# Centring a weight ahead of block sums, later bias loads, and a plan chosen from twelve

## The chip, the cores and the metric

The kernel runs on one core of a Trainium2 chip. The metric is the device time of one execution in microseconds (us). A profile of one execution says what each engine did and when. The engines are TensorE (PE, with its weight loads as PEld), VectorE (DVE), ScalarE (ACT), GpSimd (POOL) and SyncE (SP, which only issues transfers here).

## The reference

Four layers work on x of shape (64, 256, 128) with one adjacency matrix of 256 x 256. Each adds its result to its input and takes a layer norm over the last axis of 128.

```python
# layer 0: sum over powers of adj, seven weights
x = _layernorm(x + _L0(x, adj, adj, weight_1))     # x_all = [x, A x, A^2 x, A^3 x, A x, A^2 x, A^3 x]; einsum('bnik,iok->bno')
# layer 1: adj @ (x @ weight) + bias
x = _layernorm(x + _L1(x, adj, weight, bias))
# layer 2: (D^-1/2 (adj + I) D^-1/2) @ x @ W.T + b
x = _layernorm(x + _L2(x, adj, W, b))
# layer 3: five steps of a gated recurrent cell, two messages through adj
for _ in range(5):
    av = concat(adj @ h, adj @ h); u3 = h @ u3_w.T + u3_b
    z = sigmoid(av @ w3_w.T + w3_b + u3); r = sigmoid(av @ w4_w.T + w4_b + u3)
    hv = tanh(av @ w5_w.T + w5_b + (r * h) @ u5_w.T + u5_b)
    h = (1 - z) * h + z * hv
x = _layernorm(x + h)
```

All values are float32.

## The kernel before

The batch of 64 is cut into 32 groups of two (`NB`). A group's values carry the number of its first batch element: x_4 is the input of the third group. Within a group every layer follows the other; across groups twelve may be in work at once (`ACTIVE`). A value of a group is a tile of 128 x 512.

Nothing is written in a fixed order. Each piece of work is recorded as an `Op` with an engine, an assumed cost, an assumed lag until its result can be used, a rank, and a function that emits its instructions. `Plan.order` (L84) is a list scheduler: among the pieces whose inputs are assumed to be there, it takes the one that can start first and, among equals, the one of lower rank. A group's rank is its number (L468), for the last seven groups (`LEVEL`) a closer spaced one that grows with each piece; the weights' preparation has ranks of its own, from -9 to 2.1, the first argument of `pre` (L217), `fetch` (L224) and `load` (L228). The resulting list is the instruction order of each engine. Each engine takes its instructions strictly in that order and waits at the first whose inputs are missing. SP is such a queue as well: a transfer behind one that still waits is not issued. A transfer from SP uses one of eight semaphores in turn, so the ninth waits until the first has landed.

The head of the program, which the change touches, holds these pieces:

- PE warms up on transposes (L254), turns the adjacency matrix to `aT` (L270) and squares it (L277, `p_a`, copied by ACT to `a2T`, L284). The first two groups (x_0, x_2) take plain products with `a2T` and turn x on PE; the later ones use seven block products in place of eight (`seven`, L704), for which POOL forms differences (L724 to L732: `tsq`, `tqq`) and DVE adds up the parts (L751 to L761, with `mq` as the result).
- `w0s` (L291 to L296) are the sums of the seven slices of W_0 that belong to equal powers. `centre` (L300) takes the mean over the output channels off a weight, so that a later layer norm needs no mean. The centred `w0s` is what the first weight products (`py`, L565 to L597) read. `w0_blocks` (L311) forms differences of it.
- `aTp` is a copy of `aT` with its rows in another order, made by four transfers on SP (L324). `block_sums` (L359) forms five sums of a matrix's four blocks on DVE, for `aT`, `a2T`, the normalised `anT`, and `aTp`.
- `wb` (L380 to L386) holds the weight of layer 1 and the two biases, all centred by one call of `centre`. Both biases are loaded from POOL's queue (L385), behind a small DVE copy `made` that gives `wb` its first writer; six further bias columns `braw` follow on the same queue (L421).
- For group 2 on, x is turned by DVE (`tx`, L852), stored (`dx`, L855) and read back (`xT`, L860). The load of a group's x (L843) may be issued only after the first piece of the group two before it.

Of the kernel before, what the change touches and what calls it, by code (L numbers as in the profile page):

```python
# [1 line left out]

# [8 lines left out]
OP = mybir.AluOpType  # L11
AX = mybir.AxisListType

P = 128
# [3 lines left out]
LEVEL = 7  # L18
# [9 lines left out]
class Val:  # L28
# [3 lines left out]
    def __init__(self, kind, shape, name, nb=NB):  # L32
        self.kind, self.shape, self.name, self.nb = kind, shape, name, nb
        self.writers, self.readers, self.users = [], [], []
        self.slot = self.tile = None
# [15 lines left out]
class Plan:  # L51
# [3 lines left out]

    def __init__(self, slots):
        self.ops, self.slots = [], slots

    def add(self, engine, cost, lag, rank, run, reads=(), writes=(), after=(), joint=False):

# [18 lines left out]
        self.ops.append(op)  # L81
        return op

    def order(self):  # L84
        free = {}
        pool = {k: [(0.0, i) for i in range(n)] for k, n in self.slots.items()}
        left = {op: len(op.deps) for op in self.ops}
        placed = {op: [v for v in op.vals if v.kind != "const"] for op in self.ops}
        after = {op: [] for op in self.ops}
        for op in self.ops:  # L90
            for d in op.deps:
                after[d].append(op)
        open_ = {}
        ready = {}
        for op in self.ops:
            if not left[op]:
                ready.setdefault(op.engine, []).append((0.0, op))
        done = []
        while any(ready.values()):
            best = None  # L100
            for e, waiting in ready.items():
                t0 = free.get(e, 0.0)
                pick = None
                for at, op in waiting:
                    need, opens = {}, 1
                    for v in placed[op]:
                        if v.slot is None:
                            need[v.kind] = need.get(v.kind, 0) + 1
                        elif v.kind == "bank":
                            opens = 0  # L110
                    short = False
                    for k, n in need.items():
                        if len(pool[k]) < n:
                            short = True
                            break
                        at = max(at, sorted(pool[k])[n - 1][0])
                    if short:
                        continue
                    key = (max(at, t0), opens, op.rank, op.seq)
                    if pick is None or key < pick[0]:  # L120
                        pick = (key, op)
                if pick and (best is None or pick[0] < best[0]):
                    best = pick
            assert best, "the plan is stuck"
            (start, *_), op = best
            ready[op.engine] = [w for w in ready[op.engine] if w[1] is not op]
            op.start, op.end = start, start + op.cost + op.lag
            free[op.engine] = start + op.cost
            for v in placed[op]:
                if v.slot is None:  # L130
                    pool[v.kind].sort()
                    v.slot = pool[v.kind].pop(0)[1]
                    open_[v] = len(v.users)
                open_[v] -= 1
                if not open_[v]:
                    pool[v.kind].append((max(u.end for u in v.users), v.slot))
            for n in after[op]:
                left[n] -= 1
                if not left[n]:
                    at = max(d.end for d in n.deps)  # L140
                    ready.setdefault(n.engine, []).append((at, n))
            done.append(op)
        assert len(done) == len(self.ops)
        return sorted(done, key=lambda op: (op.start, op.seq))


def pe_cost(columns, n=1):
    return n * 2 * (max(columns, P) / 1.2 + 2)
# [11 lines left out]
def kernel(  # L160
# [30 lines left out]
    nc = tc.nc  # L191
    B, N, C = x.shape
    T = N // P
    G = B // NB
# [8 lines left out]
    SHAPES = {"bank": [P, 512], "x": [P, 512], "w": [P, 512], "th": [P, 384], "q": [P, P], "h": [P, 256], "st": [P, Q * 6], "mv": [P, Q * 2],  # L203
              "ve": [P, Q], "rs": [P, Q]}
    slots = {"bank": BANKS, "x": ACTIVE + 3, "w": 38, "th": 12, "q": 12, "h": 21, "dram1": 8, "dram2": 16, "st": 12, "mv": 12, "ve": 24, "rs": 12}
    plan = Plan(slots)


    def constant(name, shape):
# [7 lines left out]
    def pre(rank, engine, cost, run, reads=(), writes=(), lag=None, joint=False, after=()):  # L217
        lag = lag or {"SP": 2300, "PE": 260, "DVE": 260, "ACT": 130, "POOL": 100}[engine]
        return plan.add(engine, cost, lag, rank, run, reads, writes, after, joint)
# [3 lines left out]

    def fetch(rank, o, src, v, queue, after=()):  # L224
        e, cost = QUEUES[queue]
        return pre(rank, queue, cost, lambda: e.dma_start(o, src), [], [v], lag=8000, joint=True, after=after)

    def load(rank, name, shape, src, keep=True, queue="SP", lag=2300):  # L228
        v = constant(name, shape) if keep else Val("w", shape, name)
# [4 lines left out]
    ident = const.tile([P, P], F32, name="ident")  # L234
# [10 lines left out]
    warm = temp("warm")  # L245
# [4 lines left out]
    def warming(n):  # L250
        for i in range(n):
            nc.tensor.transpose(warm.ap[:, (i % 4) * P:(i % 4 + 1) * P], ident, ident)
# [4 lines left out]
    a_nat = load(-9, "a_nat", [P, T, N], adj.rearrange("(t p) m -> p t m", p=P), False)  # L257
    aT, a2T = constant("aT", [P, T, N]), constant("a2T", [P, T, N])
    p_at, p_a2, p_an = temp("p_at"), temp("p_a2"), temp("p_an")
# [17 lines left out]
    def square():  # L277
        for mt in range(T):
            for kt in range(T):
                mm(p_a2.ap[:, mt * N:(mt + 1) * N], a_nat.ap[:, kt, mt * P:(mt + 1) * P], aT.ap[:, kt, :],  # L280
                   kt == 0, kt == T - 1)

    pre(-8, "PE", pe_cost(N, 4), square, [a_nat, aT], [p_a2])
    pre(-8, "ACT", act_cost(512), lambda: nc.scalar.copy(flat(a2T), p_a2.ap), [p_a2], [a2T])  # L284


# [2 lines left out]
    w0s = constant("w0s", [P, 4, C])  # L289
# [9 lines left out]

    def centre(v, means):  # L300
        nc.vector.reduce_sum(means.ap, v.ap, axis=AX.X)
        nc.vector.tensor_scalar(means.ap, means.ap, -1.0 / C, None, op0=OP.mult)
        nc.vector.tensor_tensor(v.ap, v.ap, means.ap[:, :, None].to_broadcast(v.ap.shape), op=OP.add)

    w0m = constant("w0m", [P, 4])
    pre(-7, "DVE", 1500, lambda: centre(w0s, w0m), [w0s], [w0s, w0m])


    w0t = constant("w0t", [P, 4, C])
# [6 lines left out]
        nc.vector.tensor_sub(t3, w_3, w_1)  # L316
        nc.vector.tensor_sub(t4, w_2, t2)

    pre(1.2, "DVE", 1000, w0_blocks, [w0s], [w0t])


    aTp = constant("aTp", [P, T, N])
# [8 lines left out]
    ahat, anT = Val("w", [P, T, N], "ahat"), constant("anT", [P, T, N])  # L331
# [24 lines left out]

    sums_of = {}

    def block_sums(rank, name, aTs):  # L359
        v = constant(f"s_{name}", [P, 5, P])  # L360
        a11, a12, a21, a22 = (aTs.ap[:, kt, t * P:(t + 1) * P] for t in range(T) for kt in range(T))

        def run():
            nc.vector.tensor_add(v.ap[:, 0, :], a21, a22)
            nc.vector.tensor_sub(v.ap[:, 1, :], v.ap[:, 0, :], a11)
            nc.vector.tensor_sub(v.ap[:, 2, :], a11, a21)
            nc.vector.tensor_sub(v.ap[:, 3, :], a12, v.ap[:, 1, :])
            nc.vector.tensor_scalar(v.ap[:, 4, :], a22, -1.0, None, op0=OP.mult)

        pre(rank, "DVE", 1200, run, [aTs], [v])  # L370
        sums_of[aTs] = v

    block_sums(0.6, "aT", aT)
    block_sums(0.6, "a2T", a2T)
    block_sums(0.6, "anT", anT)
    block_sums(0.7, "aTp", aTp)

    wb, wbm = constant("wb", [P, 3, C]), constant("wbm", [P, 3])  # L380

    made = pre(-9, "DVE", 100, lambda: nc.vector.tensor_copy(wb.ap[:, 1:3, 0], ident[:, :2]), [], [wb])
    fetch(0.6, wb.ap[:, 0, :], w1, wb, "SP")
    for i, b in ((1, b1), (2, b2)):
        last = fetch(0.1, wb.ap[:, i, :], bass.AP(tensor=b.tensor, offset=b.offset, ap=[[0, P], [1, C]]), wb, "POOL", (made,))  # L385
    pre(0.9, "DVE", 1100, lambda: centre(wb, wbm), [wb, w0s], [wb, wbm])  # L386
    w1c, b1c, b2c = ((wb, wb.ap[:, i, :]) for i in range(3))
    raw = {name: load(0.6, f"raw_{name}", [P, src.shape[1]], src, False, lag=9000)
# [29 lines left out]
    braw, bsum = constant("braw", [P, 6]), constant("bsum", [P, 3])  # L418

    for i, src in enumerate((w3_b, w4_b, w5_b, u3_b, u3_b, u5_b)):  # L420
        fetch(0.2, braw.ap[:, i:i + 1], src.rearrange("(p o) -> p o", o=1), braw, "POOL", (last,))  # L421
    pre(0.4, "DVE", 150, lambda: nc.vector.tensor_add(bsum.ap, braw.ap[:, :3], braw.ap[:, 3:]), [braw], [bsum])
    zb, rb, hb = ((bsum, bsum.ap[:, i:i + 1]) for i in range(3))

# [24 lines left out]
    class Group:  # L449
        def __init__(self, start, nb):  # L450
            self.start, self.nb, self.first, self.last = start, nb, None, None
            self.gate = self.load_gate = ()
            self.count = 0
            self.q, self.width = nb * T, nb * N

            self.by_tile = (lambda v: v.ap.rearrange("p (k q i) -> p q k i", k=4, q=self.q),
                            lambda v: v.ap.rearrange("p (q k i) -> p q k i", k=4, q=self.q))
# [532 lines left out]
```

## Time and profile before

| what | us |
|---|---|
| three timed runs | 1344.65, 1346.7, 1347.05 (median 1346.7) |
| the profiled execution | 1345.33 |
| its span, first to last instruction | 1343.5 |
| mean granted TensorE clock | 0.996 |

The span is a little shorter than the execution's own time, since what lies around the first and last instruction is not in it. Below, every point in time is counted from the span's start. A row of instructions in order of time gives its start, its length, engine, line and operation, the tile written and the tiles read; in brackets stands how long the engine was idle before it and what ended that. The length of a DVE or ACT row holds some overlap with the next one, so the distance of two starts is the better price of an instruction in a row. A float32 matmul stands as two records, a transpose as one.

### The profile page before, as it was taken

The numbers are of one execution on the slowest core, as the hardware profiler recorded it, in microseconds if no ns is written. First come the engines' busy times: TensorE is split into PE (matmuls) and PEld (weight loads), VectorE is DVE, ScalarE is ACT, GpSimd is POOL, SyncE is SP. The second block draws the span as 40 slices with busy tenths as digits, with TensorE's granted clock in tenths as the row PEclk, the third lists the DMA queues.
The fourth block names the chain that finished last, engine by engine and source line by source line (L and its number), as shares of the span: only waits on it lengthen the run. The fifth ranks groups of instructions, "written<-read, shape, count | busy, mean of one in ns | idle before, by whom it ended". The sixth has DMA issues, their size and how long they took to land.

```text
span 1343.5 us, 22696 instructions
## 1 busy us (share of the span) xinstructions
PE 1326.7 (99%) x6913; PEld 931.0 (69%) x6913; DVE 1046.2 (78%) x2579; ACT 773.2 (58%) x2361; POOL 638.2 (48%) x998
## 2 busy tenths in 40 slices
PE   8999999999999999999999999999999999999997
PEld 6987756667677877766666767766666787666554
DVE  6976767879886978777779796986886778777776
ACT  3677645544556666554655656565555588544445
POOL 4887633434355746352535465353343476322212
PEclk8999999999999999999999999999999999999999
DMA  5521323534242333343524332333332213433323
GB/s 154 147 67 57 86 85 90 156 89 133 81 130 75 102 88 110 95 118 87 157 74 131 100 107 70 105 116 99 106 95 80 70 57 118 122 90 94 89 85 102
DMA packets 269305, 134.87 MB, mean 100 GB/s; under 512 B 175712, under 2 KB 240864, under 8 KB 269184
## 3 DMA queue, kind: packets, MB, share of 16 engines
q1 hardware_dynamic: 268928, 133.29, 34.4%
q8 instruction: 55, 0.90, 0.3%
q14 instruction: 66, 0.54, 0.1%
q0 software_dynamic: 256, 0.13, 0.1%
HBM read 67.31 MB, written 65.80 MB: 99 GB/s over the span
## 4 chain that ended last, share of the span: by engine, by line
PE 95%; DVE 2%; ACT 1%; DMA 1%; issue 0%; SPq 0%; POOLq 0%; POOL 0%; DVEq 0%; ACTq 0%
PE pr L201 30%; PE ph L201 20%; PE pmg L201 19%; PE py L201 11%; PE pm L201 7%; PE pz L201 4%; PE pmq L201 3%; DMA x<-in_x_dram 1%; PE s L201 1%; ACT y L524 0%; DVE s L546 0%; DVE tx L852 0%; DVE ss L619 0%; ACT y L539 0%; DMA aTp<-aT 0%
## 5 line engine op out<-in xcount | busy, mean ns | idle before, releaser
L201 PE MATMUL pr<-mg,w435u5T 128*128 128x512 f32 x640 | 322.3, 593 | 0.0
L725 POOL TENSOR_TENSOR tsg<-h 128x256 f32<-128x256 f32 x128 | 95.2, 743 | 285.5 <-DMA h<-dh 202.1
L528 POOL TENSOR_TENSOR rs<-ve,half 128x4 f32<-128x4 f32 x99 | 101.3, 1023 | 205.4 <-ACT y L524 169.0
L831 ACT ACTIVATE pr<-pr,bsum 128x512 f32<-128x512 f32 x160 | 105.6, 660 | 137.7 <-PE pr L201 137.2
L831 ACT ACTIVATE r<-pr,bsum 128x512 f32<-128x512 f32 x160 | 105.4, 659 | 127.2 <-PE pr L201 124.9
L524 ACT ACTIVATE y<-s,root 128x128 f32<-128x128 f32 x396 | 153.7, 393 | 17.3 <-DVE s L546 15.7
L201 PE MATMUL pr<-hT,w2u3T 128*128 128x512 f32 x320 | 163.0, 593 | 0.0
L201 PE MATMUL ph<-mg,w435u5T 128*128 128x512 f32 x320 | 162.9, 593 | 0.0
L201 PE MATMUL ph<-rh,w435u5T 128*128 128x512 f32 x320 | 162.8, 593 | 0.0
L838 DVE TENSOR_TENSOR d<-ph,hT 128x512 f32<-128x512 f32 x160 | 109.5, 685 | 67.4 <-ACT ph L831 66.8
L201 PEld LDWEIGHTS pmg<-aTp,h 128*128 128x128 f32 x512 | 91.9, 196 | 74.4 <-issue 47.6
L201 PEld LDWEIGHTS pr<-mg,w435u5T 128*128 128x128 f32 x640 | 105.7, 191 | 51.3 <-issue 40.3
L831 ACT ACTIVATE ph<-ph,bsum 128x512 f32<-128x512 f32 x160 | 105.3, 658 | 57.5 <-PE ph L201 56.1
L838 DVE TENSOR_TENSOR rh<-r,hT 128x512 f32<-128x512 f32 x160 | 108.8, 681 | 33.9 <-ACT r L831 30.5
L539 ACT ACTIVATE y<-s,rs 128x128 f32<-128x128 f32 x384 | 122.1, 394 | 9.4 <-POOL rs L528 9.1
L838 DVE TENSOR_TENSOR pr<-pr,d 128x512 f32<-128x512 f32 x157 | 108.4, 691 | 1.3
L838 DVE TENSOR_TENSOR hT<-hT,pr 128x512 f32<-128x512 f32 x157 | 106.8, 680 | 1.7
L201 PE MATMUL pmg<-s_aTp,tsg 128*128 128x128 f32 x768 | 106.7, 275 | 0.0
L872 POOL TENSOR_TENSOR yb<-y,wb 128x512 f32<-128x512 f32 x64 | 83.0, 1297 | 43.5 <-ACT y L539 40.4
L201 PE MATMUL pmg<-aTp,h 128*128 128x128 f32 x512 | 98.4, 279 | 0.0
L201 PEld LDWEIGHTS ph<-rh,w435u5T 128*128 128x128 f32 x320 | 58.0, 190 | 57.1 <-issue 42.7
L201 PEld LDWEIGHTS pmg<-s_aTp,tsg 128*128 128x128 f32 x768 | 95.8, 192 | 0.0
(202 smaller groups left out, 2808.5 us busy)
## 6 DMA issues: line engine op xcount, KB each, us to landing
dh<-th SPq DMA_DIRECT2D x160, 256.0 KB, 2.0
h<-dh SPq DMA_DIRECT2D x256, 128.0 KB, 2.5
x<-in_x_dram SPq DMA_DIRECT2D x32, 256.0 KB, 3.3
hT<-dh SPq DMA_DIRECT2D x128, 64.0 KB, 2.0
out_dram<-y SPq DMA_DIRECT2D x32, 256.0 KB, 2.4
dx<-tx SPq DMA_DIRECT2D x30, 256.0 KB, 2.5
xT<-dx SPq DMA_DIRECT2D x60, 128.0 KB, 2.9
dn<-tn SPq DMA_DIRECT2D x29, 256.0 KB, 2.0
```

What stands on the lines that cost most here:

```text
L201: nc.tensor.matmul(o, lhsT, rhs, start=start, stop=stop, skip_group_check=shared)
L524: nc.scalar.activation(nat(y)[:, q, :], nat(s)[:, q, :], AF.Square, scale=C ** -0.5, bias=root[:, 0:1], accum_out=ve.ap[:, q:q + 1])
L528: nc.gpsimd.tensor_tensor(rs.ap, ve.ap, half[:, :self.q], op=OP.pow)
L539: nc.scalar.mul(nat(y)[:, q, :], nat(s)[:, q, :], rs.ap[:, q:q + 1])
L725: nc.gpsimd.tensor_tensor(ts.ap[:, :2 * P].rearrange("p (x c) -> p x c", x=2), ins(h)[:, 1], ins(h)[:, :, 0], op=OP.subtract)
L831: self.act(lambda: nc.scalar.activation(t.ap, ps.ap, func, bias=bias[1], scale=1.0), [ps, bias[0]], [t], act_cost(self.width) + 100)
L838: self.dve(lambda: nc.vector.tensor_tensor(out(t), way(a), way(b), op=op), [a, b], [t])
L872: nc.gpsimd.tensor_tensor(nat(yb), nat(y), bias[1][:, None, :].to_broadcast([P, self.q, C]), op=OP.add)
```

## The change

There are six edits.

1. `centre` multiplies by -1/C and adds in one `scalar_tensor_tensor` in place of a `tensor_scalar` on the means and an addition. It is called for `w0s` (512 elements a partition) and `wb` (384).
2. The sums of `anT` and `aTp` are recorded as dependent on the centring of `w0s`, and `w0_blocks` gets rank 0.2 in place of 1.2.
3. `made` copies two columns of `w0s` instead of the identity, so both bias loads from POOL can begin only when `w0s` is there; their ranks go from 0.1 to 0.5, those of the six columns from 0.2 to 0.55, and the assumed lag of all from 8000 to 5000 ns.
4. Two more warming transposes follow the square of the adjacency matrix.
5. `order` makes twelve plans. The first uses the ranks as they are, the others add a random number to each rank, up to 0.4, or up to 0.01 where the rank is at least 25 (the last seven groups). The plan with the earliest assumed end is kept. A plan that gets stuck is dropped.
6. `Plan` is told the rank from which the smaller random number applies.

```diff
+    def order(self, tries=12):
+        best, rng = None, random.Random(1)
+        for _ in range(tries):
+            for op in self.ops:
+                op.place = op.rank + (rng.uniform(0, 0.4 if op.rank < self.ends else 0.4 / 40) if best else 0)
+                for v in op.vals:
+                    v.slot = None
+            done = self.attempt()
+            if done:
+                span = max(op.end for op in done)
+                if best is None or span < best[0]:
+                    best = span, done, {v: v.slot for op in done for v in op.vals}
+        for v, slot in best[2].items():
+            v.slot = slot
+        return best[1]
...
-                    key = (max(at, t0), opens, op.rank, op.seq)
+                    key = (max(at, t0), opens, op.place, op.seq)
...
-    plan = Plan(slots)
+    plan = Plan(slots, G - LEVEL)
...
-        return pre(rank, queue, cost, lambda: e.dma_start(o, src), [], [v], lag=8000, joint=True, after=after)
+        return pre(rank, queue, cost, lambda: e.dma_start(o, src), [], [v], lag=5000, joint=True, after=after)
...
-    pre(-8, "PE", pe_cost(N, 4), square, [a_nat, aT], [p_a2])
+        warming(2)
+    pre(-8, "PE", pe_cost(N, 4) + 220, square, [a_nat, aT], [p_a2, warm])
...
-        nc.vector.tensor_scalar(means.ap, means.ap, -1.0 / C, None, op0=OP.mult)
-        nc.vector.tensor_tensor(v.ap, v.ap, means.ap[:, :, None].to_broadcast(v.ap.shape), op=OP.add)
+        nc.vector.scalar_tensor_tensor(v.ap, means.ap[:, :, None].to_broadcast(v.ap.shape), -1.0 / C, v.ap,
+                                       op0=OP.mult, op1=OP.add)
...
-    pre(-7, "DVE", 1500, lambda: centre(w0s, w0m), [w0s], [w0s, w0m])
+    centred = pre(-7, "DVE", 1600, lambda: centre(w0s, w0m), [w0s], [w0s, w0m])
...
-    pre(1.2, "DVE", 1000, w0_blocks, [w0s], [w0t])
+    pre(0.2, "DVE", 1000, w0_blocks, [w0s], [w0t])
...
-        pre(rank, "DVE", 1200, run, [aTs], [v])
+        pre(rank, "DVE", 1200, run, [aTs], [v], after=after)
...
-    block_sums(0.6, "anT", anT)
-    block_sums(0.7, "aTp", aTp)
+    block_sums(0.6, "anT", anT, (centred,))
+    block_sums(0.7, "aTp", aTp, (centred,))
...
-    made = pre(-9, "DVE", 100, lambda: nc.vector.tensor_copy(wb.ap[:, 1:3, 0], ident[:, :2]), [], [wb])
+    made = pre(-7, "DVE", 100, lambda: nc.vector.tensor_copy(wb.ap[:, 1:3, 0], w0s.ap[:, :2, 0]), [w0s], [wb])
...
-        last = fetch(0.1, wb.ap[:, i, :], bass.AP(tensor=b.tensor, offset=b.offset, ap=[[0, P], [1, C]]), wb, "POOL", (made,))
+        last = fetch(0.5, wb.ap[:, i, :], bass.AP(tensor=b.tensor, offset=b.offset, ap=[[0, P], [1, C]]), wb, "POOL", (made,))
...
-        fetch(0.2, braw.ap[:, i:i + 1], src.rearrange("(p o) -> p o", o=1), braw, "POOL", (last,))
+        fetch(0.55, braw.ap[:, i:i + 1], src.rearrange("(p o) -> p o", o=1), braw, "POOL", (last,))
```

What this does to the engines' queues at the head, as the built program has it:

- DVE: after the sums of `w0s` come at once the mean and the fused instruction; then one sum of a recurrent weight, the turn of x_4 (`tx`), the two-element copy, `w0_blocks`, two more weight sums, the sums of `aTp`, a weight difference, the scaling of the adjacency rows, the turns of x_6 and x_8, the difference `sd` of xT_4, the centring of `wb`, the turn of x_10, the scaling to `anT`, the turn of x_12, the sums of `anT`, and then the additions that end in `mq` of x_4.
- POOL: no load at the start. The differences of x_4, the two loads of biases, the differences of x_6 and x_8, three loads of columns, `rs` of the first group, two loads, the first `ts`, `yb`, the second `ts`, one load.
- SP: the eight weight loads before the transfers of `aTp` stand in another order. The loads of x_4 and x_6 follow `aTp` as before; then dx_4, x_8, xT_4, dx_6, x_10, dx_8, x_12, xT_6, xT_8. Before it was dx_4, x_8, dx_6, x_10, xT_4, xT_6.
- PE: the same sequence up to the first products with `w0s` but for the two transposes; behind them the order differs slightly from the first row on, and so it does on all engines through most of the run. The last products, and what follows them on ACT, POOL, DVE and SP, stand in the same order.

More of the change, by code (lines that the diff above doesn't have):

```diff
@@ L1 @@
+import random
 from contextlib import ExitStack
@@ L51, with __init__ @@
 class Plan:
-    def __init__(self, slots):
-        self.ops, self.slots = [], slots
+    def __init__(self, slots, ends):
+        self.ops, self.slots, self.ends = [], slots, ends
     def add(self, engine, cost, lag, rank, run, reads=(), writes=(), after=(), joint=False):
@@ L82, in add, with attempt @@
         return op
-    def order(self):
+    def order(self, tries=12):
[13 more added lines that the diff above has]
+        return best[1]
+    def attempt(self):
         free = {}
@@ L123, in order @@
                     best = pick
-            assert best, "the plan is stuck"
+            if not best:
+                return None
             (start, *_), op = best
@@ L142, in order @@
             done.append(op)
-        assert len(done) == len(self.ops)
         return sorted(done, key=lambda op: (op.start, op.seq))
@@ L357, with block_sums @@
     sums_of = {}
-    def block_sums(rank, name, aTs):
+    def block_sums(rank, name, aTs, after=()):
         v = constant(f"s_{name}", [P, 5, P])
```

## Prediction

> **What bounds the kernel now.** I read the page's busy shares first, then TensorE's waits, the table of stretches, and the DVE and PE rows of the first 40 us in order of time.
>
> ```profile
> PE 1326.7 (99%) x6913; PEld 931.0 (69%) x6913; DVE 1046.2 (78%) x2579; ACT 773.2 (58%) x2361; POOL 638.2 (48%) x998
> ```
>
> PE is busy for 99% of the span, so the matmuls themselves set the time; only what PE loses can be won, 16.8 us of visible idle. The waits name where:
>
> ```profile
> PE py L201 <- DVE w0s L303: 4.9, 1, 4.9
> PE warm L252 <- POOL ident masks.py:199: 1.4, 1, 1.4
> PE pmq L201 <- DVE mq L757: 1.2, 1, 1.2
> PE pm L201 <- ACT us L767: 0.7, 2, 0.6
> ```
>
> The one large wait is for the centred W_0. The stretches show the rest (start:end, length, busy us of PE, PEld, DVE, ACT, POOL, granted clock, DMA share, GB/s):
>
> ```profile
> 12.50:17.50 5.00, 0.06 (x2) 0.04 (x1) 3.14 (x9) 0.59 (x1) 1.40 (x2) 0.83 0.46 131
> 17.50:22.70 5.20, 5.20 (x13) 4.18 (x14) 5.10 (x14) 0.37 (x1) 2.27 (x5) 0.51 0.00 0
> 34.50:40.00 5.50, 3.75 (x31) 3.40 (x31) 5.42 (x16) 3.23 (x15) 3.65 (x6) 1.00 0.89 240
> 450.00:465.00 15.00, 14.04 (x95) 11.16 (x94) 14.00 (x34) 9.34 (x34) 11.43 (x19) 1.00 0.21 65
> ```
>
> Three things are to be seen. After the wait PE runs at clock 0.51 for 5.2 us: six pairs of 256-column matmuls start 0.86 apart there and 0.43 apart later, so this costs 6 x 0.43 = 2.6 us though PE counts as busy. From 34.5 to 40 DVE is busy 5.42 of 5.5 us and PE only 3.75: there DVE's queue is the bound. And far into the run an order of groups costs about 1 us (450 to 465). The tail (last matmul to the end, 7.9 us) is a chain ACT, POOL, DVE, DMA whose order is unchanged.
>
> **The edits at the head.**
>
> *Centring before the aTp sums.* DVE now:
>
> ```profile
> 9.74 0.99 DVE L294 TENSOR_TENSOR w0s<-w_raw 128x128 f32<-128x128 f32 x3
> 14.26 0.29 DVE L364 TENSOR_TENSOR s_aTp<-aTp 128x128 f32<-128x128 f32 x1 [3.53 <-DMA aTp<-aT]
> ...
> 15.33 0.68 DVE L301 TENSOR_REDUCE w0m<-w0s 128x4 f32<-128x512 f32 x1
> 16.04 0.17 DVE L302 TENSOR_SCALAR w0m<-w0m 128x4 f32<-128x4 f32 x1
> 16.25 1.09 DVE L303 TENSOR_TENSOR w0s<-w0s,w0m 128x512 f32<-128x512 f32 x1
> ```
>
> The sums of W_0 end at 10.73, then DVE stands 3.53 us for the transfer of aTp. In the new order the mean follows at once: 10.73 + 0.68 = 11.41, then the fused instruction. Its price is not in the trace. The row of an undisturbed 512-element add (L838) is 0.684; the 1.09 above ran beside POOL's first L725. [...] By the row w0s is ready at 12.1[...]. The second x's product keeps PE until 10.66 + 8 x 0.216 = 12.39, so with 0.15 us from DVE to PE (17.34 to 17.49 now) the wait is 0 or 0.4. I take 0.3. First use of w0s moves from 17.49 to about 12.7: 4.8 us; with no idle stretch there the 2.6 us of half clock go too. **PE arrives 7.4 us earlier** at all that follows, until something else is late.
>
> *Two warming transposes after the square*: 2 x 0.112 = 0.22, in the 0.24 PE stands for a2T at 8.15; the copy waits on the square's last matmul alone. Nothing; 0.22 if that cover goes. *The two-element copy* moves from the idle DVE start (0.17) to behind the first tx: 0.1, counted below.
>
> **What is late next: DVE, at the first seven-product block, that of the third group (x_4).** PE must wait there for L757 (the 1.2 us wait now). From py's start to that point the new PE order holds 24 256-column matmuls (two records of 0.216 each: 10.4), 15 of 128 columns (0.223: 3.35) and 9 transposes (0.112: 1.0), so PE stands there at 12.7 + 14.7 = 27.4. DVE, in its new order, with spacings of the rows now: x_4 lands at 15.99 (its issue stays behind the aTp transfers at 12.64); tx 1.06 -> 17.1; copy 0.1; w0t 0.93; two weight sums 1.1; aTp sums 1.07; w34 0.2; ahat rows 0.93; tx 1.06 -> 22.5. SP sends dx_6 and the load of x_10 only behind that tx; a load lands 3.05 to 4.3 later, 26.0 to 27.2. Meanwhile tx_8 -> 23.5; sd waits for xT_4, whose two issues stand on SP behind the landing of dx_4: 17.1 + 2.1 to 3.1, then 1.1, then 3.6 to 4.9, so about 25.0; sd, bias centring -> 26.2; tx_10 to 27.3 to 28.3; anT 0.8; tx_12 1.04 -> 29.1 to 30.2; anT sums 1.07 (the aTp row) to 3.08 (31.26 to 34.34 now, L366 alone 1.36 while POOL's L872 ran); the five short ones to L757 1.45. Sum: PE goes on between 31.8 and 34.9, against 35.91 now. POOL's L872 falls on anT this time, a softer neighbour on the sums, so I take 33.8: **2.1 us earlier**, and 5.3 of the 7.4 are given back.
>
> That stall is 6.4 us, and the clock fell 3.2 us into the idle of now (12.55 to 15.78), so it falls again: at most 2.6 us, nothing if DVE feeds PE slowly anyway (34.5 to 40). I take half, 1.3. **Head: -0.8** (ends: -4.1 and +1.6).
>
> *POOL.* The eight bias loads leave 1.83 to 9.5, where POOL stood, and now lie between the differences of the first groups: two behind tqq_4, three ahead of group 0's rs, three behind it. Now one costs 0.55, also at 8.43 and 8.97 while DVE's a2T sums (two SBUF inputs) ran: 4.4 us in all. By that, tsq work goes on to 23.1, the three end at 24.8, rs 25.8, ts from 27.0: not later than the DVE chain. The b loads are issued by 19.1 and land 3.7 to 6.5 later, by 25.6; sd ends 25.4. [...] I take the row[...].
>
> **The order of the run.** Every rank gets a random part (0.4, or 0.01 in the last seven groups) and the shortest of twelve plans is kept, so PE's order differs from the head to near the end. Work is equal: 2 transposes more. What can change is PE's lost time between 40 and 1335 us. From the starts of its rows, beyond 0.112, 0.216 and 0.43 us a record: 1.4 in 450 to 460, 1.2 in 1100 to 1120, 0.5 at 66, 0.3 at 500, 0.5 in 710 to 790, so 3.9 us of removable waits. The planner's costs agree with the trace (512 columns 857 ns against 0.86; an ACT copy of 512 592 against 587), so a plan that is shorter in them should have fewer such waits; but landings scatter (L843: 3.05 to 4.6 at the head) and new waits can arise. Ends -3.5 and +1.5; I take **-1.5**. The lower lag of 5000 for bias loads only moves the consumers, counted above.
>
> **Sum.** -0.8 - 1.5 = -2.3. The profiled execution took 1345.33 (span 1343.5 and 1.8 around it): 1343.0. The three runs' median, 1346.7, lies 1.4 above; the mean of all four is 1345.9, and I forecast from that: **1343.6 us**. A run scatters by about a microsecond; 0.2% (2.7 us) is about what a measurement can tell from no change.
>
> **Rivals.** *The head saving arrives whole* (7%): DVE or the transfers keep up, -7.4 -1.5: 1337. For it: the wait and the slow clock are real; against: DVE's own row count above. *Hidden anyway* (18%): the new stall and its slow clock eat all, and the new order has as many waits as the old: 1345.9. For: DVE is full from 34.5 to 40. *Slower* (5%): [...] Place: POOL from 17.9. [...] It decides once a wb load on POOL takes over 2.5 us or lands after 27. *Forecast* (70%): 1342 to 1345.5; the shown median stands 0.8 above my base, so 55 of these 70 fall below 1344.0 and 15 within 0.2%. Faster 0.55 + 0.07 = 0.62, same 0.15 + 0.18 = 0.33, slower 0.05. Range 1340.5 to 1346.6: it leaves out the whole-saving and slow cases and takes in the rest.
>
> **What would show it.** PE's first py at 12.4 to 12.8 without the 4.9 us wait, at full clock; [...] a new PE wait of 4 to 7 us ending at 32 to 35 on DVE L757 (L776 in the new file), with a clock under 1 behind it; wb loads of 0.55 on POOL; PE idle after 40 us under 1.5. The forecast is wrong if that wait is under 3 us (then below 1341), or if waits far into the run sum to over 4 us.

## The result, and the profile after

The changed kernel took 1342.37 us in the median of nine runs (1341.5 to 1344.61). The kernel before, on the same chip, took 1347.05 (nine runs, 1344.65 to 1347.35). The ratio is 0.997, with a 95% interval of 0.996 to 0.998. A second set of runs gave 1342.75 against 1346.6, ratio 0.9971 [0.9959, 0.9982]. The gain is thus 3.9 to 4.7 us, and 1343.6 was forecast.

The profiled execution took 1342.32 (span 1340.5). The busy shares first:

```profile
PE 1325.7 (99%) x6915; PEld 931.9 (70%) x6915; DVE 1039.0 (78%) x2577; ACT 773.6 (58%) x2361; POOL 636.1 (47%) x998
```

PE's busy time is 1326.7 - 1325.7 = 1.0 us less with two records more, so the work is the same; of the 3.0 us by which the span is shorter, 2.0 are idle time. TensorE's waits after the change (us in total, times, longest):

```profile
PE pmq L219 <- DVE mq L776: 5.1, 1, 5.1
PE warm L270 <- POOL ident masks.py:199: 1.4, 1, 1.4
PE pz L219 <- DVE u L664: 1.0, 1, 1.0
PE pm L219 <- ACT us L786: 0.4, 1, 0.4
```

The 4.9 us wait for `w0s` is gone, and a wait of 5.1 for `mq` has come, where 1.2 stood before. The stretches (start:end, length, busy us of PE, PEld, DVE, ACT, POOL, granted clock, DMA share, GB/s) show where:

```profile
12.50:17.50 5.00, 5.00 (x25) 4.32 (x24) 4.27 (x11) 1.23 (x3) 3.51 (x6) 1.00 0.58 175
17.50:22.70 5.20, 5.20 (x30) 4.64 (x29) 5.17 (x10) 2.82 (x12) 4.87 (x10) 1.00 0.62 91
22.70:34.50 11.80, 6.68 (x46) 6.28 (x45) 9.55 (x21) 5.42 (x21) 7.47 (x11) 0.85 0.87 244
34.50:40.00 5.50, 5.14 (x34) 4.85 (x33) 3.88 (x14) 2.23 (x8) 0.87 (x1) 0.69 0.71 189
...
450.00:465.00 15.00, 15.00 (x87) 10.96 (x87) 12.28 (x30) 10.03 (x35) 9.38 (x16) 1.00 0.43 123
```

From 12.5 to 22.7 PE is full at clock 1.00; before it was busy for 5.26 of these 10.2 us, 5.20 of them at clock 0.51. From 22.7 to 34.5 it has 6.68 of 11.8, where it had all; then the clock is low (0.69 from 34.5 to 40). And the wait in 450 to 465 is gone.

Idle rows and half clock are best added in one number. The table takes the distance of each PE row's start to the next and subtracts the row's own price (0.112, 0.216, 0.43 us for 128, 256, 512 columns, by the median distances in both traces); what is left is lost. The prices are rounded, and some 6700 records stand after 50 us, so nearly 3 us of that column are rounding, the same in every kernel: read its differences, not its level. Rows that start more than 0.01 us late sum to 4.0 and 3.9 after 50 us in the two profiles of before, and to 0.9 and 1.3 in those of the changed kernel. Each kernel was profiled twice; the second profile of each is that of the experiments `e11_before_again` and `e8_after_again`.

| PE's lost time, us | 0 to 12 | 12 to 25 | 25 to 50 | after 50 | sum |
|---|---|---|---|---|---|
| before (run of 1345.33) | 2.7 | 7.7 | 2.3 | 6.7 | 19.4 |
| before again (1346.97) | 3.7 | 8.1 | 2.6 | 6.7 | 21.0 |
| changed (1342.32) | 3.2 | 0.0 | 9.4 | 3.8 | 16.3 |
| changed again (1342.37) | 2.5 | 0.0 | 9.7 | 4.2 | 16.4 |

From means of two profiles: 7.9 are won between 12 and 25 us, 7.1 are given back between 25 and 50, 0.4 are won in the first 12, and 2.7 after 50. That makes 3.9, the gain of the second set of runs. Most of what stays comes from far into the run.

The giving back is read from DVE's rows (start, length, line, operation, written tile, read tiles; in brackets the idle time before, and what ended it):

```profile
11.46 0.69 DVE L320 TENSOR_REDUCE w0m<-w0s 128x4 f32<-128x512 f32 x1
12.18 0.69 DVE L321 SCALAR_TENSOR_TENSOR w0s<-w0m,w0s 128x512 f32<-128x512 f32 x1
...
17.03 0.81 DVE L383 TENSOR_TENSOR s_aTp<-aTp 128x128 f32<-128x128 f32 x1
...
19.62 0.28 DVE L413 TENSOR_TENSOR both_w<-both_w,both_w 128x128 f32<-128x128 f32 x1
...
26.11 1.13 DVE L871 STREAM_TRANSPOSE tx<-x 128x512 f32<-128x512 f32 x1 [1.79 <-DMA x<-in_x_dram]
27.17 0.82 DVE L366 TENSOR_SCALAR anT<-p_an,dinv 128x256 f32<-128x256 f32 x2
28.27 1.08 DVE L871 STREAM_TRANSPOSE tx<-x 128x512 f32<-128x512 f32 x1 [0.28 <-DMA x<-in_x_dram]
...
29.77 1.65 DVE L385 TENSOR_TENSOR s_anT<-anT 128x128 f32<-128x128 f32 x1
...
32.74 0.28 DVE L776 TENSOR_TENSOR mq<-wsq,pmq 128x128 f32<-128x128 f32 x1
```

PE's row behind it:

```profile
33.07 0.80 PE L219 MATMUL pmq<-s_a2T,x 128*128 128x128 f32 x2 [5.12 <-DVE mq L776]
```

`w0s` is ready at 12.8. PE has nothing to do from 27.9 on until `mq` of x_4 is there, but L776 is reached at 32.74: DVE stands 1.79 us for x_10, then works through turns, the scaling to `anT` and its five sums, of which one takes 1.65 in place of 0.28, while POOL runs two L744. POOL issues the two loads of biases ahead of that:

```profile
15.56 0.72 POOL L244 DMA_DIRECT2D wb<-in_L_gnn_b_dram  x1
16.28 0.54 POOL L244 DMA_DIRECT2D wb<-in_L_gnn_bias_dram  x1
```

### The profile page after: what moved, and what is told of

The parts are those of the page before. It is cut to its first block, busy times and chain, and to the rows that moved or that the text cites. A ratio compares the mean times of both kernels' runs of the same rounds, so it can differ in the third digit from the quotient of the medians.

```text
span 1340.5 us, 22669 instructions
## 1 busy us (share of the span) xinstructions
PE 1325.7 (99%) x6915; PEld 931.9 (70%) x6915; DVE 1039.0 (78%) x2577; ACT 773.6 (58%) x2361; POOL 636.1 (47%) x998
## 4 chain that ended last, share of the span: by engine, by line
PE 97%; DVE 1%; DMA 1%; issue 0%; SPq 0%; ACT 0%; POOLq 0%; POOL 0%; ACTq 0%
PE pr L219 31%; PE ph L219 21%; PE pmg L219 19%; PE py L219 11%; PE pm L219 8%; PE pz L219 4%; PE pmq L219 3%; DMA x<-in_x_dram 1%; PE s L219 1%; DVE tx L871 0%; SPq L345 0%; DVE sd L635 0%; ACT y L543 0%; POOLq L1004 0%; DVE both_w L411 0%
## 5 line engine op out<-in xcount | busy, mean ns | idle before, releaser
L744 POOL TENSOR_TENSOR tsg<-h 128x256 f32<-128x256 f32 x128 | 94.0, 735 | 281.1 <-DMA h<-dh 200.4
L219 PEld LDWEIGHTS pr<-mg,w435u5T 128*128 128x128 f32 x640 | 108.8, 191 | 70.3 <-issue 57.6
L780 DVE TENSOR_TENSOR mg<-pmg,usg 128x256 f32<-128x256 f32 x160 | 66.6, 418 | 39.7 <-PE pmg L219 38.3
```

The costliest lines, as they stand in the source:

```text
L219: nc.tensor.matmul(o, lhsT, rhs, start=start, stop=stop, skip_group_check=shared)
L744: nc.gpsimd.tensor_tensor(ts.ap[:, :2 * P].rearrange("p (x c) -> p x c", x=2), ins(h)[:, 1], ins(h)[:, :, 0], op=OP.subtract)
L780: nc.vector.tensor_tensor(o(m, slice(1, 3)), o(ps, slice(1, 3), False), both, op=OP.add)
```

## The experiments

Each was compared with runs of the kernel before on its own chip: e1 to e4 with a median of 1346.13 (65 runs), e5 to e8 with 1346.6 (28 runs), e9 to e12 with 1346.63 (22 runs). The edits of e1, e2, e5, e9, e10 and e12 act where the pieces are emitted, after the planner, so that nothing else in the order moves; e3, e4, e6 and e7 change the planner itself. `named` finds a piece by the tiles that it touches, and `...` marks lines left out. The changed kernel itself was timed for the result and again beside e5 to e7; its distance from the other experiments compares two chips. A profile is of one execution, and need not be the median one: that of e3 took 1346.55, that of e7 1342.55, both about 2 above the median.

### e1: the centring alone

The kernel before, in its own order; only the centring of `w0s` comes ahead of the sums of `aTp`.

```diff
-        for op in plan.order():
+        ops = plan.order()
...
+        mean = next(op for op in ops if op.engine == "DVE" and named(op, "w0s", "w0m"))
+        sums = next(op for op in ops if op.engine == "DVE" and named(op, "s_aTp"))
+        ops.remove(mean)
+        ops.insert(ops.index(sums), mean)
+        for op in ops:
```

> The kernel before with one thing moved: on VectorE the centring of w0s stands ahead of the five sums of aTp; every other instruction keeps its place, so the order of the run beyond the head is the old one. Theory A (the saving at the head is given back in VectorE's queue): PE's first py moves from 17.5 to about 13 us, at full clock, but PE then waits 5 us or more for L757 at the first seven-product block and the time falls by 0 to 2 us (1345 to 1347 beside 1347.05 for the kernel before); waits beyond 40 us stay at some 4 us. Theory B (the head is worth its visible wait and slow clock): the time falls by 7 us, to 1340.

Measured: 1344.77, ratio 0.9989 [0.9983, 0.9996], a gain of 1.4. The addition in its centring, with nothing on POOL beside it, and its longest wait:

```profile
12.45 0.69 DVE L303 TENSOR_TENSOR w0s<-w0s,w0m 128x512 f32<-128x512 f32 x1
```

```profile
PE pmq L201 <- DVE mq L757: 4.8, 1, 4.8
```

The wait for `w0s` turned into one of 4.8 for `mq`, with nothing else of the change in place. Lost time was 0.2 between 12 and 25 us and 8.0 between 25 and 50, and 6.7 after 50 as before. The exchange of one wait for the other belongs to the centring alone. Theory A, with a wait a little under its 5.

### e2: the eight bias loads early again

The changed kernel, its eight bias loads on POOL put back to the start (`made` copies the identity again).

```diff
...
+        two = [op for op in ops if op.engine == "POOL" and len(op.vals) == 1 and named(op, "wb")]
+        six = [op for op in ops if op.engine == "POOL" and len(op.vals) == 1 and named(op, "braw")]
+        ops = [made, *two, *(op for op in ops if op is not made and op not in two and op not in six)]
+        at = 1 + next(i for i, op in enumerate(ops) if op.engine == "POOL" and named(op, "dinv"))
+        ops[at:at] = six
...
```

> The changed kernel with the eight bias loads back at the start of GpSimd's queue (the two-element copy takes two columns of the identity again), all other instructions in the changed order. Theory A (the two bias loads slow the head's transfers): the load of W_0 lands at 9 us again (6.96 in the changed kernel), x_4 at 16 (13.75), the first py starts near 13 all the same, and PE's wait for L776 ends about 2 us later; the time rises by 1 to 2 us, to 1343.5 to 1344.5. Theory B (the later loads only keep GpSimd free): landings stay within 0.5 us of the changed kernel's, and the time stays at 1342.4 or falls by up to 1 us, since GpSimd has 4.4 us less in front of the first ts.

Measured: 1344.31, ratio 0.9985 [0.9979, 0.9992], 1.6 to 1.9 above the changed kernel: theory A. The list of DMA issues (count, KB each, us from issue to landing) has for the 448 KB of W_0, first in the changed kernel, then here:

```profile
w_raw<-in_L_gnn_weight_dram SPq DMA_DIRECT2D x1, 448.0 KB, 5.2
```

```profile
w_raw<-in_L_gnn_weight_dram SPq DMA_DIRECT2D x1, 448.0 KB, 9.0
```

W_0 lands at 10.74 in place of 6.96. SP's queue stands for it: its next issue comes at 10.76 in place of 6.98, and x_4 lands at 17.43 in place of 13.75. PE loses 3.9 in the first 12 us and 1.7 in the next 13, where the changed kernel lost 2.5 to 3.2 and nothing.

### e3: one plan in place of twelve

The changed kernel with `tries=1`.

```diff
-    def order(self, tries=12):
+    def order(self, tries=1):
```

> The changed kernel with one plan in place of twelve: ranks without a random part, all edits at the head kept. Theory A (most of the gain comes from the order of the run): the head is like the changed kernel's (no wait for w0s, then one of 5 us for VectorE), PE's waits beyond 40 us are 3 to 5 us in place of 1.5 or so, and the time is 1344.5 to 1347. Theory B (most comes from the head): the time is 1342 to 1343, like the changed kernel's.

Measured: 1344.79, ratio 0.9988 [0.9982, 0.9995], 2.0 to 2.4 above the changed kernel. All the other edits together are thus worth 1.3. Its waits:

```profile
PE pmq L219 <- ACT usq L786: 6.5, 2, 6.3
...
PE pr L219 <- DVE mg L780: 0.8, 1, 0.8
PE py L219 <- DVE v L664: 0.7, 1, 0.7
PE pm L219 <- DVE m L776: 0.6, 1, 0.6
```

Theory A. The last three fall after 50 us (lost time there 7.2); the large one is in the head, longer than with the chosen plan.

### e4: the twelve plans alone

The kernel before with the new `order`, `attempt` and `Plan(slots, G - LEVEL)`, none of the other edits.

> The kernel before with the twelve plans alone; no edit at the head. Theory A (most of the gain comes from the order of the run): the wait for w0s of about 5 us and the slow clock stay, waits beyond 40 us fall to 1 to 3 us, and the time is 1343 to 1345. Theory B (most comes from the head): 1346 to 1347.5.

Measured: 1346.51, ratio 1.0002 [0.9994, 1.001]. The forecast gain is missed: lost time after 50 us is 6.7, as before, only at other places. The choice among twelve is worth 2.2 in the changed kernel and nothing here.

### e6 and e7: other random numbers

The changed kernel with `random.Random(2)` and `random.Random(4)` in place of `random.Random(1)`, so that another plan is kept.

> The changed kernel with another sequence of random numbers in the plans, so that another plan of twelve is kept. Theory A (a plan that is shorter by the planner's costs has fewer waits on the chip, whichever it is): 1342 to 1343.5, with PE's lost time after 50 us under 4.5. Theory B (what the kept plan brings is chance: the waits depend on landings and lengths that the planner doesn't know): anything from 1341 to 1346, and the lost time after 50 us like that of the single plan, 6 to 7, in about half of such sequences.

> As the one before with a third sequence of random numbers. Theory A (shorter plans have fewer waits): 1342 to 1343.5, lost time after 50 us under 4.5. Theory B (chance): 1341 to 1346, and not in the order in which the planner ranks the kept plans.

Measured: 1344.65, ratio 0.9986 [0.9979, 0.9992], with 2; and 1340.51, ratio 0.9958 [0.9945, 0.997], with 4. Lost time after 50 us is 6.6 and 3.5. The ends that the planner itself assumes for the kept plans, in its own costs, are 1317.1 (one plan), 1315.3 (as changed), 1315.5 (with 2), 1316.2 (with 4), and 1314.2 in e4; measured were 1344.8, 1342.4 to 1342.8, 1344.7, 1340.5 and 1346.5. The shortest of the five by the planner (e4, with another head) is the slowest on the chip, and the fastest is the fourth. Within the changed kernel none of the three chosen plans is slower than the single one, but their order is not the planner's, and one of them gains nothing. So theory A falls; theory B's chance fits, though 1340.51 is below what either named. What makes one draw better than another was not found.

### e8: the changed kernel again

> The changed kernel once more, beside the next three on one chip, so that they are compared with it directly. Theory A (the gain is real: about 1.4 from the centring moved ahead, 1.9 from the later bias loads, the rest from the order chosen): 1342.4, ratio to before 0.996 to 0.998, and the profile again shows no wait for w0s, one wait of about 5.1 for L776 and PE's lost time after 50 us under 4. Theory B (the first set of runs was a good one for it): 1344 or more, ratio above 0.998.

Measured: 1342.75, and the profile of the table above; its wait for L776 was 5.6. Theory A holds for the time; lost time after 50 us, 4.2, is a little over its 4. Its split of the gain is not shown by this run: alone, the centring gained 1.4 and the later loads 1.9 (e12), but all edits at the head together 1.3 (e3), so the parts do not add up.

### e5 and e10: DVE's queue relieved

Two orders of the changed kernel. In e5 the five sums of `anT` come behind the first `mq` of x_4; in e10 also the turn of x_12 and two differences `sd`, each with what depends on it. `post13` is the piece of L776; `put_behind` moves a piece, and those that hang on it or share its buffers, behind the goal.

```diff
...
+        late = next(op for op in ops if op.engine == "DVE" and named(op, "s_anT"))
+        ops.remove(late)
+        first = next(op for op in ops if op.engine == "DVE" and op.run.__name__ == "post13")
+        ops.insert(ops.index(first) + 1, late)
...
```

```diff
...
+        goal = next(op for op in ops if op.engine == "DVE" and op.run.__name__ == "post13" and named(op, "mq_4"))
+        for name in ("sd_8", "sd_6", "s_anT", "tx_12"):
+            put_behind([next(op for op in ops if op.engine == "DVE" and named(op, name))], goal)
```

> The changed kernel with one piece moved on DVE: the five sums of anT (3.1 us by the rows of the changed kernel's profile) come behind the first mq of x_4 instead of ahead of it. Theory A (DVE's queue at the first seven-product block of x_4 is what takes the head's saving back): the wait for L776 shrinks from 5.1 to 2 to 3, the clock stays full or is at half for a shorter time, and the time falls by 2 to 4, to 1338.5 to 1340.5. Theory B (PE would wait at the next piece anyway, since the transfers and the other DVE pieces of the next groups are as late): the wait is only cut in pieces, the lost time of the first 50 us stays at 12 to 13, and the time stays at 1342 to 1343.

> The changed kernel with four pieces moved on DVE behind the first mq of x_4 (L776): the turn of x_12, the five sums of anT, and the two differences sd that wait for xT of x_6 and x_8. Then only the turn of x_10 and the scaling to anT stand between the centred biases and that mq. Theory A (DVE's queue is the bound of the head): mq of x_4 is written at about 28.5 instead of 33, the wait for it is under 1.5, the clock stays full, and the time falls by 3 to 4.5, to 1338 to 1339.5. Theory B (the head has too little work for PE until the turned x of the later groups has come back): the wait is split, PE's lost time in the first 50 us falls by less than 1.5, the clock falls to half as before, and the time is 1341 to 1342.7.

Measured: e5 1342.54, ratio 0.9974 [0.9962, 0.9985]; e10 1342.13, ratio 0.9967 [0.9955, 0.998]. Neither can be told from the changed kernel. Lost time in the first 50 us is 11.8 and 12.3, against 12.5 and 12.2 in the two profiles of the changed kernel. The waits of e5, then of e10:

```profile
PE pmq L219 <- DVE mq L776: 3.9, 1, 3.9
...
PE pz L219 <- DVE u L664: 1.1, 1, 1.1
PE pmq L219 <- ACT usq L786: 0.5, 1, 0.5
```

```profile
PE pmq L219 <- ACT usq L786: 3.2, 1, 3.2
PE pmq L219 <- DVE mq L776: 1.8, 1, 1.8
```

In e10 the first `mq` was written at 29.28, 3.5 us earlier, and the wait for it fell to 1.8; a new one of 3.2 follows, so 5.0 in all. Its DVE and ACT rows tell why:

```profile
29.28 0.29 DVE L776 TENSOR_TENSOR mq<-wsq,pmq 128x128 f32<-128x128 f32 x1
29.48 1.10 DVE L871 STREAM_TRANSPOSE tx<-x 128x512 f32<-128x512 f32 x1
...
32.10 0.75 DVE L635 TENSOR_TENSOR sd<-xT 128x256 f32<-128x256 f32 x2
32.77 0.28 DVE L770 TENSOR_TENSOR usq<-usq,pmq 128x128 f32<-128x128 f32 x1
```

```profile
33.09 0.27 ACT L791 COPY mq<-pmq 128x128 f32<-128x128 f32 x1 [4.55 <-DVE usq L770]
```

The moved pieces now stand ahead of L770 of x_6; ACT waits for that at L791, and behind L791 stands the copy that PE needs. DVE stood 1.84 us for x_10 and had no gap from its landing at 26.8 to 33, so a piece moved from one place holds up the next. Theory B's numbers came, but its reason is not shown: in these rows the cause is still DVE's queue, one block further on.

### e9: the same on the faster plan

The kernel of e7; the turn of x_10, for whose transfer DVE stood 2.57 us, comes behind the first `mq` of x_8.

```diff
...
+        goal = next(op for op in ops if op.engine == "DVE" and op.run.__name__ == "post13" and named(op, "mq_8"))
+        put_behind([next(op for op in ops if op.engine == "DVE" and named(op, "tx_10"))], goal)
```

> The kernel with the third sequence of random numbers (1340.51), with one piece moved on DVE: the turn of x_10, which held DVE's queue for 2.57 us until x_10 had landed and then took 1.09, comes behind the first piece of mq of x_8 (L776) instead of ahead of it. Theory A (a single piece at the head of DVE's queue makes PE's 5.7 us wait): the wait shrinks to 2 to 3, PE's lost time in the first 50 us falls from 12.96 to 10 or less, the time to 1337.5 to 1339. Theory B (PE has no other work there, since what the next groups need is as late): the wait shrinks by about 3, but others of together 2 to 3 follow, and the time stays within 1 of 1340.5.

Measured: 1340.67, ratio 0.9954 [0.9941, 0.9966]; e7 had 1340.51. The wait in e7, then the waits here:

```profile
PE pmq L219 <- DVE mq L776: 5.7, 1, 5.7
```

```profile
PE pmq L219 <- DVE mq L776: 3.2, 1, 3.2
...
PE pz L219 <- DVE se L641: 1.1, 1, 1.1
```

The wait fell from 5.7 to 3.2, and 1.1 of it came back at once; lost time in the first 50 us is 11.9 against 13.0. The profile is better, the timed runs are not: a gain of 1 is not seen in five runs of each. Theory B. e7 and e9 ran on different chips. These two kernels are the fastest of the study; e7's five runs (1339.44 to 1342.55) and the six of the changed kernel beside it (1342.2 to 1343.23) overlap a little.

### e11: the kernel before again

> The kernel before, for a second profile. Its profiled execution took 1345.33, its median is 1346.1 to 1347. Theory A (that execution was a lucky one in the clock or in some landing): 1346 to 1347.5, with PE's lost time 0.7 to 2 above 19.4, most of it in the first 50 us. Theory B (the profile is typical and the timed runs lose time elsewhere): 1345.3 again, lost time 19.4.

Measured: 1346.97. Lost time is 1.6 above the first profile's, all in the first 50 us: W_0 landed at 10.28 in place of 9.31, all of SP's transfers behind it followed, and full clock was granted at 7.20 in place of 5.54. The execution shown ahead of the prediction was a lucky one. Theory A.

### e12: the bias loads late, alone

The kernel before, in its own order; the two loads of `wb` come behind `tqq` of x_4, the six columns after 30 us, and the centring of `wb` ahead of the scaling to `anT`. The sum of the columns moves as well, to just ahead of its first use.

```diff
...
+        loads = [op for op in ops if op.engine == "POOL" and len(op.vals) == 1 and op.vals[0].name in ("wb", "braw")]
...
+        for op in loads:
+            ops.remove(op)
+        at = ops.index(on("POOL", "tqq_4")) + 1
+        ops[at:at] = loads[:2]
+        for op, host in zip(loads[2:], [op for op in ops if op.engine == "POOL" and op.start > 30000][::2]):
+            ops.insert(ops.index(host) + 1, op)
```

> The kernel before, in its own order, with the eight bias loads on POOL moved: the two of wb come behind the differences tqq of x_4, the six columns after 30 us, and the centring of wb comes behind the turn of x_8. Theory A (two loads [...] at the start hold up the head's transfers): w_raw lands at about 7.0 instead of 9.3, x_4 at 13.8 instead of 16.0, the wait for w0s ends at about 15.2 instead of 17.5, and the time falls by 1 to 2. Theory B (the early loads cost nothing; the landings of the changed kernel are earlier for another reason, such as the order of SP's loads): w_raw lands at 9 to 10 and the time stays within 0.5 of before.

Measured: 1344.78, ratio 0.9986 [0.9978, 0.9993], a gain of 1.9. SP's first loads stand in the same order as before. Its transfer of W_0, and its wait:

```profile
w_raw<-in_L_gnn_weight_dram SPq DMA_DIRECT2D x1, 448.0 KB, 6.0
```

```profile
PE py L201 <- DVE w0s L303: 4.0, 1, 4.0
```

W_0 lands at 7.74 in place of 9.31, x_4 at 14.20 in place of 15.99. `w0s` comes at 16.3, less early than expected (15.2): POOL's differences now run beside more of the centring (L302 takes 0.58 in place of 0.17). Theory A: the early loads held up the head's transfers.

Which of the eight do so, the DMA packets in the traces tell in part. W_0 is 128 packets of 3584 bytes. At 6.25 us, 73 to 100 of them were done in the five profiles with early loads (88 in the first of before), and 112 to 127 in the nine with late ones (119 in the first of the changed kernel). No packet of a column starts before 7.7 us; the 32 packets of the two loads of `wb`, 4096 bytes each, start at 4.6 to 8.1 us in the kernel before. So the delay begins with the two loads of `wb`. Whether the columns add to it is not shown.

## Why the prediction was near, and which terms were off

- **The bound.** PE is full before and after, and the gain is lost time. Right.
- **Wait and slow clock at `w0s`: 7.4 us.** The two pairs of profiles show 7.9 between 12 and 25 us. Right. The first `py` began at 12.38 in the second profile, as named (12.4 to 12.8), and at 13.09 in the first, where full clock was granted only at 7.17 (5.36 in the second) and the products ahead of it ran late.
- **The fused instruction.** Its row is 0.69, and 0.61 lie between its start and the next; the plain addition of the same tile, undisturbed in e1, has the same 0.69. So it has the price of the row (0.684). The small wait that I allowed (0.3, between 0 and 0.4) rested on a slower price, which no run shows; it did not come: PE's product before it ran to 13.09 in the first profile, when `w0s` was there.
- **Two warming transposes.** Nothing, as said; the 0.2 us wait for `a2T` is gone, because they fill it.
- **What is late next.** Right in place, engine and line: PE stood from 27.9 to 33.07 for L776; 27.4 and 33.8 were predicted. The half clock came again, from 31.07 to 37.9, and cost 2.1 by the excess of the rows in it (1.3 predicted, at most 2.6). Given back are 7.1, against 5.3 + 1.3 = 6.6. The size owes something to luck: x_4 landed 2.2 us earlier than in my chain (see the bias loads), but the sums of `aTp`, put at 1.07, took 2.6 (17.03 to 19.62) while POOL ran its differences. The turn of x_6 so ended at about 21.9 (22.5 predicted), and x_10, whose issue stands behind it, landed at 26.09 (26.0 to 27.2 predicted); from there the chain ran as told.
- **The head.** -0.8 was predicted. The profiles show 7.1 - 7.9 = -0.8 after 12 us and -0.4 ahead of it; e3, with all edits but the plans, gained 1.3. Right in sign and nearly in size.
- **POOL's bias loads.** Two were issued at 15.56 and 16.28 and took 0.72 and 0.54, beside DVE's sums with two SBUF inputs (L334 to L336 and L411, from 15.33 on). At the start of the kernel before, beside an idle DVE, they took the same. So the slower rival fell, whose mark was a load over 2.5 us; that DVE's work slows POOL's loads is not shown by any run. They landed at 19.5 and 20.8, well ahead of 25.6. But a term was missing: I let x_4 land at 15.99 as before, since its issue stood behind `aTp`; it landed at 13.75. Taking eight early loads away freed the transfers of the head, worth 1.9 (e12) when nothing else is changed. In the changed kernel putting them back costs 1.6 to 1.9 (e2).
- **The order of the run: -1.5.** This is the mis-sized term. Measured are -2.7 by lost time after 50 us (6.7 to 4.0) and -2.0 to -2.4 by e3. It was inside the ends I gave (-3.5 and 1.5), but my reason for it was weak: that a plan shorter in the planner's costs has fewer waits is not borne out by e4, e6 and e7.
- **The base: 1345.9.** The mean of four runs, one of them the lucky one of 1345.33. Longer series have 1346.1 to 1347.05. With 1346.6 and -2.3 the forecast would have been 1344.3. So the sum erred by 1.6 to 2.4 in the change (mostly the order, and the 0.4 of the first 12 us), and the low base took 0.7 of this back: that part of the nearness is luck.
- **The rivals.** The head saving did not arrive whole: the new wait is over 5 us. Nor was it all eaten. The signs named for a wrong forecast (that wait under 3 us, over 4 us of waits far into the run) did not appear: in the count by which the prediction found 3.9 us of waits far into the run, the changed kernel has 0.9 and 1.3. PE's visible idle after 40 us, named as under 1.5, was 1.0 and 1.6.
- **One slip** that carries no weight: from the end of the last matmul to the end of the span are 7.1 us, not 7.9.

What stays open: what the six columns add to the slowing by the two loads of `wb` (they were only moved together), why the kernel before gains nothing from twelve plans, and whether the head's wait can go at all. No run gave PE other work there. Nor did one, in the changed kernel's own order, fill the 1.79 us that DVE stands for x_10 (e9 took that stand away in another order, for no gain in time): the scaling to `anT` and its five sums, 3.2 us as they ran, stand behind that turn, though PE had written the input `p_an` by 22.3.

## What to carry to other kernels

When a wait goes, follow the next engine's queue in order up to the next point where the bound engine needs it; here, moving single pieces of a full queue only moved the wait by one block. A list scheduler's shorter plan is a draw, not a gain: try several draws on the chip and keep the one that measures best. Small loads that nobody needs early were not free at the start, even on another queue (1.6 to 1.9 us for eight of them here): look at when the large transfers beside them land.

## What the runs showed of the hardware

- **Early small loads.** In the five profiles with the eight loads at the start, W_0 landed at 9.2 to 10.74; in the nine with late loads at 6.65 to 7.92. The 448 KB took 7.4 to 9.0 us against 4.9 to 6.2, though the two loads of `wb` bring 64 KB each, and the six columns 0.5 KB each.
- **The half clock in the head.** It lasted 6.83 us in the first profile of either kernel: from 15.78 to 22.61 before, after 10.24 us at full clock, and from 31.07 to 37.90 in the changed one, after 23.89. PE's rows of 128 columns started 0.21 apart in the latter, in place of 0.112. In nine of the other twelve profiles the granted clocks of the stretches from 12.5 to 40 us add up to 6.7 to 7.0 us at half clock; in e2, e7 and e9 the clock is 0.50 to 0.54 in the last of these stretches. The longest wait in the head was 3.2 to 6.3 us in all fourteen.
- **DVE beside POOL.** The third sum of `anT` on DVE (L385, two SBUF inputs), 0.28 in e10, where POOL ran nothing beside it, took 1.65 while POOL ran two L744, and 0.81 to 1.36 in six other profiles. In the changed kernel the next DVE row starts at 31.33, just behind the end of POOL's two L744 (29.86 + 1.39 = 31.25).
